# Two-level products in the last two blocks, modulation in place, and a second load of x, in a one-core adaLN + FFN kernel

## The chip, the cores and the metric

The kernel runs on 1 NeuronCore of one Trainium2 chip. The metric is the device time of one execution in microseconds (us). Five engines run their own instruction queues in order: TensorE (PE; its weight loads are listed apart, as PEld), VectorE (DVE), ScalarE (ACT), GpSimd (POOL) and SyncE (SP), which here only issues DMAs. An engine that waits on a semaphore holds up all that is queued behind it.

## The reference

x has 64 batches of 64 rows of 512 (float32), cond has 64 rows of 256.

```python
# modulation and first product
q_emb = relu(q @ W3 + b3)                        # 64 x 512
v_sum = sum(v, axis=1, keepdims=True)            # over the 64 rows of a batch
x1 = (n * v + v_sum) * q_emb[:, None, :]
y  = relu(x1 @ W2 + b2)                          # 4096 x 512 @ 512 x 512
# second product, with a shared and six routed low-rank experts (rank 16, top 2)
base   = y @ W_base + b_base                     # 4096 x 512 @ 512 x 512
shared = (y @ A_s) @ B_s
gates  = softmax(y @ W_router + b_router)        # top 2 of 6, as weights w_per_e
routed = einsum(einsum(y, A_r) * w_per_e, B_r)
out = x + base + shared + routed
```

## The kernel before

Features lie on the 128 partitions (chunks of 128: NC = 4), tokens in the free dimension. The 4096 tokens are cut into NB = 4 blocks (k = 0 to 3) of 1024, a block into two halves h of TB = 512 tokens. Each block has a first product (x1 @ W2, relu to y), then `ph` (y with the 118 columns of A_s, A_r and the router, L801), then `second` (y @ W_base, plus the routed part through `pt`, `hwT` and `bcat_sb`).

Both 512 x 512 products are done by Strassen-Winograd: of the two token halves and two feature halves come 7 products instead of 8. `weight_sums` and `row_sums` make the sums of operands on DVE (`t2`, `tb` for the weights; `s` of the modulated x, `sy` of y); `product(ps, i, j, ...)` is number i of the seven for output chunk j: two matmuls of 128 columns of weights with 512 tokens, accumulated in a PSUM bank. Seven products share four banks named x, y, w and z; what several outputs have in common (p1, u) is carried over by ACT copies and DVE adds. There are six banks for all this (`ps_p`).

- Block 0 (`first_mixed`): the first half of its tokens without Strassen as the data arrives, the rest with seven products.
- Blocks 1 and 2 (`first_seven`): seven products on one level.
- Block 3 (`first_inner`): two levels. Each of the seven products is again done by seven, on 256 tokens (`q(n, t)`): 49 matmuls instead of 28. Here p1, y and z are seeded by ACT copies from PSUM to PSUM (`seed_y`, `seed_z`), and PE adds onto the copy. The sums of the inner level are `inner_t` (weights), and `first`, `sums` and `late` (x); `inner_t`, `first` and `sums` are made during block 2, `late` at the start of block 3.

The order of the work on each engine is the order in which the code issues it (a manual schedule). The modulation of block k+1 is laid between the work of block k by hand: `modulate` makes a list of steps (per chunk a sum over each batch's rows on DVE, then 16 ACT instructions, one for each batch), `prepare` puts these and the row sums of the next block into the list `behind`, `fill(n)` issues the next n steps of it, and `share()`, called nine times in `second`, issues its part of what is left. So an ACT copy or relu that PE waits for may stand behind modulations, and a DVE add behind sums.

`second` first issues the gate (softmax and top 2: three DVE steps, an Exp on ACT, nine DVE steps), then products 1, 6, 7, 2 for j=0, 1, 4, 6, 7 and so on. It takes the residual from x still in SBUF: `add_u` makes u = p1 + y on DVE, and POOL adds x to three copies of it (L662); `add_r` adds product 7; `finish` adds PSUM, bias and the copy with x on DVE (L674) and issues the output DMA on SP.

Pools: three buffers for x, two for v (the modulated x; `inner_s` takes one of them in block 3), one each for `u`, `u22`, `u21`, `u12`, which both products use in turn.

Of the kernel before, what the change touches and what calls it, by code (L numbers as in the profile page):

```python
# [27 lines left out]
NQ = Q // P  # L28
G = E + 1
# [5 lines left out]
def adaln_ffn(ctx: ExitStack, tc: tile.TileContext, xa, x0, x1, head, w3, w2, wb, a, bcat, br, outT):  # L35
# [12 lines left out]
    vpool = ctx.enter_context(tc.tile_pool(name="v", bufs=2))  # L48
    mid = ctx.enter_context(tc.tile_pool(name="mid", bufs=1))
    tmp = ctx.enter_context(tc.tile_pool(name="tmp", bufs=1))  # L50
    tmp1 = ctx.enter_context(tc.tile_pool(name="tmp1", bufs=1))
# [4 lines left out]
    outTv = outT.rearrange("k c h p t -> p c k h t")  # L56
    xs, vs, ss = {}, {}, {}

    def load_x(k):
        xs[k] = xpool.tile([P, NC, 2, TB], F32, tag="x", name=f"x_{k}")  # L60
        for c in range(NC):
            nc.sync.dma_start(xs[k][:, c].rearrange("p h t -> p (h t)"), x1[k - 1, c])
# [4 lines left out]

    def rows(k, f, h):

        return first_rows(f)[:, :, h] if k == 0 else split(xs[k][:, f, h])  # L70

    def split(t, g=2):
        return t.rearrange("p (g n) -> p g n", g=g)
# [50 lines left out]
    load_x(2)  # L124
# [9 lines left out]
    def weight_sums(w, name):  # L134

        b11, b12 = w[:, :KH, :DH], w[:, :KH, DH:]
        b21, b22 = w[:, KH:, :DH], w[:, KH:, DH:]
        all_t = const.tile([P, 4, KH, DH], F32, tag=name, name=name)
        t = [all_t[:, i] for i in range(4)]
        steps = [  # L140
            lambda: nc.vector.tensor_tensor(t[0], b12, b11, ALU.subtract),
            lambda: nc.vector.tensor_tensor(t[1], b22, t[0], ALU.subtract),
            lambda: nc.vector.tensor_tensor(t[2], b22, b12, ALU.subtract),
            lambda: nc.vector.tensor_tensor(t[3], b21, t[1], ALU.subtract),
        ]
        return {1: b11, 2: b21, 3: b22, 4: t[3], 5: t[0], 6: t[1], 7: t[2], "sums": all_t}, steps

# [25 lines left out]
    def modulate(k):  # L173


        vs[k] = v = vpool.tile([P, NC, 2, TB], F32, tag="v", name=f"v_{k}")
        vsum = small.tile([P, NC, BB], F32, tag="vsum", name=f"vsum_{k}")
        nq = small.tile([P, NC, BB], F32, tag="nq", name=f"nq_{k}")

        def sums(c):  # L180
            xc = xs[k][:, c].rearrange("p h (b n) -> p b h n", n=NH)
# [5 lines left out]
        def batches(c, lo, hi):  # L187
            for b in range(lo, hi):
                nc.scalar.activation(  # L189
                    v[:, c, :, ts(b, NH)], xs[k][:, c, :, ts(b, NH)], AF.Identity,  # L190
                    bias=vsum[:, c, b : b + 1], scale=nq[:, c, b : b + 1],
                )

        n = BB // 4
        parts = [(c, lo) for c in range(NC) for lo in range(0, BB, n)]
        steps = [lambda: sums(0)]
        for m, (c, lo) in enumerate(parts):
            if lo == 0 and c + 1 < NC:
                steps.append(lambda c=c, lo=lo: (sums(c + 1), batches(c, lo, lo + n)))
            else:  # L200
                steps.append(lambda c=c, lo=lo: batches(c, lo, lo + n))
        return steps
# [39 lines left out]
    def row_sums(a, name, cols=slice(0, TB)):  # L242

        a11, a12, a21, a22 = a[:, :KH, 0, cols], a[:, KH:, 0, cols], a[:, :KH, 1, cols], a[:, KH:, 1, cols]
        all_s = mid.tile([P, 4, KH, TB], F32, tag=name, name=name)
        s = [all_s[:, i, :, cols] for i in range(4)]
        steps = [
            lambda: nc.vector.tensor_tensor(s[0], a21, a22, ALU.add),
            lambda: nc.vector.tensor_tensor(s[1], s[0], a11, ALU.subtract),
            lambda: nc.vector.tensor_tensor(s[2], a11, a21, ALU.subtract),  # L250
            lambda: nc.vector.tensor_tensor(s[3], a12, s[1], ALU.subtract),
        ]
        return {1: a11, 2: a12, 3: s[3], 4: a22, 5: s[0], 6: s[1], 7: s[2], "sums": all_s}, steps

    def temps(name):
        return {n: tmp.tile([P, KH, TB], F32, tag=n, name=f"{n}_{name}") for n in ("u", "u22", "u21", "u12")}
# [3 lines left out]
    def fill(n):  # L260
        for _ in range(min(n, len(behind))):
            behind.pop(0)()

    def prepare(k):
        behind.extend(modulate(k))
        ss[k], steps = row_sums(vs[k], "s")
        behind.extend(steps)
        if k == NB - 1:
            prepare_inner(k)

    def prepare_inner(k):


        vectors = nc.vector.tensor_tensor
        t_flat = xpool.tile([P, NC, 2, TB], F32, tag="x", name="inner_t").rearrange("p c h t -> p (c h t)")
        at = {i: n for n, i in enumerate((5, 6, 7, 4, 1, 2, 3))}
        inner_t = t_flat[:, : 4 * 7 * P].rearrange("p (n o m) -> p n o m", n=4, o=7)

        def t_of(o, n):
            w, a = t2[o], at[o]  # L280
            b = {1: w[:, 0, :P], 2: w[:, 1, :P], 3: w[:, 1, P:]}
            return b[n] if n in b else inner_t[:, {5: 0, 6: 1, 7: 2, 4: 3}[n], a]

        w_low = w2_sb.rearrange("p (o k) m -> p o k m", k=KH)
        groups = ((slice(0, 4), lambda c, m: t2["sums"][:, :, c, ts(m, P)]),
                  (slice(4, 6), lambda c, m: w_low[:, :, c, ts(m, P)]),
                  (slice(6, 7), lambda c, m: t2[3][:, c, ts(m, P)].unsqueeze(1)))
        t_steps = []
        for o, b in groups:
            t = [inner_t[:, n, o] for n in range(4)]  # L290
            t_steps += [
                lambda t=t, b=b: vectors(t[0], b(0, 1), b(0, 0), ALU.subtract),
                lambda t=t, b=b: vectors(t[1], b(1, 1), t[0], ALU.subtract),
                lambda t=t, b=b: vectors(t[2], b(1, 1), b(0, 1), ALU.subtract),
                lambda t=t, b=b: vectors(t[3], b(1, 0), t[1], ALU.subtract),
            ]
        for n, step in enumerate(t_steps):
            m, other = 2 + n, behind[2 + n]
            behind[m] = lambda step=step, other=other: (other(), step())

        R2 = TB // 2
        s = {}

        def places():
            s["sums"] = vpool.tile([P, NC, 2, TB], F32, tag="v", name="inner_s").rearrange(
                "p c h t -> p (c h t)").rearrange("p (n o t) -> p n o t", n=4, o=4)
            s["first"] = small.tile([P, 4, 1, R2], F32, tag="inner_s1", name="inner_s1")

        def late_places():
            late = mid.tile([P, 4, KH, TB], F32, tag="sy", name="inner_late").rearrange("p n k t -> p (n k t)")  # L310
            s["late"] = late[:, : 8 * R2].rearrange("p (n o t) -> p n o t", n=4, o=2)
            s["e3"] = late[:, 8 * R2 : 12 * R2].rearrange("p (j t) -> p j t", j=KH)

        sources = (("first", lambda c, r: vs[k][:, c, 0, ts(r, R2)].unsqueeze(1)),
                   ("sums", lambda c, r: ss[k]["sums"][:, :, c, ts(r, R2)]),
                   ("late", lambda c, r: vs[k][:, KH + c, :, ts(r, R2)]))
        s_steps = [places]
        for g, a in sources:
            s_steps += [
                lambda g=g, a=a: vectors(s[g][:, 0], a(0, 1), a(1, 1), ALU.add),  # L320
                lambda g=g, a=a: vectors(s[g][:, 1], s[g][:, 0], a(0, 0), ALU.subtract),
                lambda g=g, a=a: vectors(s[g][:, 2], a(0, 0), a(0, 1), ALU.subtract),
                lambda g=g, a=a: vectors(s[g][:, 3], a(1, 0), s[g][:, 1], ALU.subtract),
            ]
        behind.extend(s_steps[:-4])
# [3 lines left out]
        def s_of(o, n):  # L329
# [7 lines left out]
        inner.update(t=t_of, s=s_of, e3=lambda: s["e3"], late=[late_places] + s_steps[-4:])  # L337
# [4 lines left out]
    def first_mixed(y):  # L342
# [3 lines left out]
        vs[0] = v = vpool.tile([P, NC, 2, TB], F32, tag="v", name="v_0")  # L346
# [12 lines left out]
        def without_sums(c):  # L359
            for j in range(KH):  # L360
                nc.tensor.matmul(
                    px[j], w2_sb[:, c, ts(j, P)], v[:, c, 0, other], start=(c == 0), stop=(c % KH == KH - 1),
                    skip_group_check=True,
                )
            if c == KH - 1:
                for j in range(KH):
                    nc.scalar.copy(p1[j], px[j])
# [5 lines left out]
        px = [ps_p.tile([P, cols], F32, tag="pp", name=f"yx_0_{j}") for j in range(KH)]  # L373
        p1 = [mid.tile([P, cols], F32, tag=f"p1_{j}", name=f"p1_0_{j}") for j in range(KH)]
        for c in range(NC):
# [9 lines left out]
            if c == NC - 1:  # L385
                modulate_scalar(v, vsum, nq, c, half, BB)
            if c > 1:
                without_sums(c - 2)
        for f in range(NC):
            nc.scalar.activation(y[:, f, :, :cols], p0[f], AF.Relu, bias=b2_sb[:, f : f + 1])  # L390
        for c in range(NC - 2, NC):
            without_sums(c)
        for step in t2_steps + s_steps:
            step()
        behind.extend(tb_steps)
        prepare(1)
        fill(1)
        for j in range(KH):
            relu(y, j, 0, px[j], other)
        pairs = temps("0")  # L400
        for j in range(KH):
            f1, f2 = j, KH + j
            bank = lambda n: ps_p.tile([P, cols], F32, tag="pp", name=f"y{n}_0_{j}")
            temp = lambda n: pairs[n][:, j, :cols]
            py, pw, pz = bank("y"), bank("w"), bank("z")
            u, r, r1, r2 = temp("u"), temp("u22"), temp("u21"), temp("u12")
            product(py, 6, j, t2, s)
            nc.vector.tensor_tensor(u, py, p1[j], ALU.add)
            product(pw, 5, j, t2, s)
            nc.vector.tensor_tensor(r, pw, u, ALU.add)  # L410
            product(pz, 7, j, t2, s)
# [12 lines left out]
    def first_seven(k, y):  # L424
# [4 lines left out]
        for j in range(KH):  # L429
# [4 lines left out]
            p1 = tmp1.tile([P, TB], F32, tag="p1", name=f"p1_{k}_{j}")  # L434
            u, r, r1, r2 = temp("u"), temp("u22"), temp("u21"), temp("u12")
# [427 lines left out]
```

## Time and profile before

| | |
|---|---|
| three runs, median (lowest, highest) | 265.69 us (265.42, 267.63) |
| the profiled execution | 265.05 us, of which 263.3 us from the first to the last instruction (the span) |
| granted TensorE clock | 0.999 |
| busy: PE, DVE, ACT, POOL | 257.9, 168.4, 119.2, 43.8 us |
| DMA | 20.13 MB moved, 76 GB/s over the span |

The stages on PE, from the chain that ended last (us from the span's start):

| block | first product and ph | second product |
|---|---|---|
| 0 | 5.6 to 40.7 | 40.7 to 72.7 |
| 1 | 72.7 to 104.3 | 104.3 to 136.1 |
| 2 | 136.1 to 167.7 | 167.7 to 199.5 |
| 3 | 199.5 to 228.1 | 228.1 to 259.3, and 4 us of adds and output |

A float32 matmul leaves two records in the trace. Records overlap in the pipeline, so the time that one costs is read from the spacing of starts (the chain's pieces), not from its own duration: four records of 512 columns take 1.72 us, six of 256 columns 1.29 us. The same holds for ACT: a modulation has a mean of 429 ns, but eight in a row take 2.65 us.

### The profile page before, as it was taken

What the parts mean: (1) busy time and instruction counts of PE and PEld (TensorE: products, weight loads), DVE (VectorE), ACT (ScalarE), POOL (GpSimd) and SP (SyncE); (2) the same over time, 40 slices, a digit from 0 to 9 for tenths busy, and PEclk for the clock granted to TensorE, in tenths of its full rate; (3) what the DMA queues carried; (4) which work ended last, traced back from release to release, by engine and by line L of the source; (5) the groups of instructions that cost most, each with busy time, mean ns of one, the idle gap of its engine ahead of it and who ended that gap; (6) DMA issues with size and microseconds to landing.
All of it is one profiled execution on the core that took longest, in us unless ns stands there. A gap on an engine that the chain in (4) does not pass through costs nothing.

```text
span 263.3 us, 2789 instructions
## 1 busy us (share of the span) xinstructions
PE 257.9 (98%) x920; PEld 148.8 (57%) x920; DVE 168.4 (64%) x296; ACT 119.2 (45%) x318; POOL 43.8 (17%) x45
## 2 busy tenths in 40 slices
PE   7999999999999999999999999999999999999995
PEld 3756895454444458444444447744446889845542
DVE  2896889636755448714667776876989566872422
ACT  2499389594018992245003998246004328101000
POOL 1000000570000000435000000055600070045300
PEclk9999999999999999999999999999999999999999
DMA  6999300004362000002220000000332000000323
GB/s 200 364 346 410 123 0 0 0 2 159 115 249 113 0 2 0 1 0 88 111 105 18 0 0 0 2 0 0 113 128 80 1 4 0 0 4 0 120 90 109
DMA packets 10303, 20.13 MB, mean 76 GB/s; under 512 B 1216, under 2 KB 3008, under 8 KB 10288
## 3 DMA queue, kind: packets, MB, share of 16 engines
q1 hardware_dynamic: 10000, 19.82, 20.7%
q8 instruction: 7, 0.11, 0.2%
q10 hardware_dynamic: 288, 0.13, 0.2%
q14 instruction: 8, 0.07, 0.1%
HBM read 11.56 MB, written 8.39 MB: 76 GB/s over the span
## 4 chain that ended last, share of the span: by engine, by line
PE 91%; ACT 5%; DMA 2%; DVE 1%; SPq 0%; issue 0%; DVEq 0%
PE oz L150 11%; PE ox L150 10%; PE ph L801 10%; PE ow L150 9%; PE py L354 5%; PE yw L150 5%; PE yz L150 5%; PE oy L150 5%; PE ia L480 5%; PE ow L668 5%; PE yx L150 4%; PE ib L480 4%; PE yy L150 3%; ACT v L189 3%; PE ox L668 3%; PE oz L668 3%
## 5 line engine op out<-in xcount | busy, mean ns | idle before, releaser
L189 ACT ACTIVATE v<-x,vsum,nq 128x64 f32<-128x64 f32 x192 | 66.3, 429 | 6.7 <-DVE vsum L185 6.7
L662 POOL TENSOR_TENSOR u_o<-u_o,x 128x512 f32<-128x512 f32 x24 | 31.9, 1356 | 178.3 <-DVE u_o L658 178.3
L801 PEld LDWEIGHTS ph<-a_sb,y 128*128 128x128 f32 x256 | 29.5, 192 | 1.8 <-issue 1.0
L801 PE MATMUL ph<-a_sb,y 128*128 128x118 f32 x256 | 29.9, 276 | 0.3 <-ACT y L340 0.3
L150 PE MATMUL ox<-y,wb_sb 128*128 128x512 f32 x64 | 29.5, 593 | 0.0
L340 ACT ACTIVATE y<-u,head_sb 128x512 f32<-128x512 f32 (+1 forms) x26 | 15.9, 633 | 8.8 <-DVE u L412 3.6
L150 PEld LDWEIGHTS ox<-y,wb_sb 128*128 128x128 f32 x64 | 11.8, 190 | 12.9 <-issue 12.9
L674 DVE SCALAR_TENSOR_TENSOR u_o<-ow,head_sb,u_o 128x512 f32<-128x512 f32 x14 | 10.5, 748 | 8.5 <-PE ow L668 8.2
L658 DVE TENSOR_TENSOR u_o<-oy,op 128x512 f32<-128x512 f32 x8 | 5.5, 688 | 15.5 <-PE oy L150 15.5
L354 PE MATMUL py<-v,w_sb 128*128 128x512 f32 (+1 forms) x40 | 14.4, 510 | 0.9 <-DMA w_sb<-in_w_dram 0.9
L150 PE MATMUL oz<-y,tb 128*128 128x512 f32 x32 | 15.1, 595 | 0.0
L150 PE MATMUL yx<-v,w_sb 128*128 128x512 f32 x32 | 15.0, 592 | 0.0
L150 PE MATMUL oz<-sy,tb 128*128 128x512 f32 x32 | 15.0, 592 | 0.0
L150 PE MATMUL oy<-sy,tb 128*128 128x512 f32 x32 | 15.0, 592 | 0.0
L437 ACT COPY p<-yx 128x512 f32<-128x512 f32 x4 | 2.3, 576 | 27.7 <-PE yx L150 27.7
L184 DVE TENSOR_REDUCE vsum<-x 128x16 f32<-128x1024 f32 x12 | 14.5, 1212 | 0.0
L654 ACT COPY op<-ox 128x512 f32<-128x512 f32 x8 | 4.7, 581 | 19.1 <-PE ox L150 19.1
L150 PE MATMUL ow<-sy,tb 128*128 128x512 f32 x28 | 13.2, 593 | 0.0
L150 PE MATMUL ow<-sy,wb_sb 128*128 128x512 f32 x28 | 13.2, 592 | 0.0
L674 DVE SCALAR_TENSOR_TENSOR x<-ox,head_sb,x 128x512 f32<-128x512 f32 x8 | 6.0, 749 | 10.6 <-PE ox L668 10.6
L486 ACT COPY ib<-ia 128x256 f32<-128x256 f32 x7 | 2.5, 357 | 21.2 <-PE ia L480 21.2
L237 ACT ACTIVATE v<-x,vsum,nq 128x64 f32<-128x64 f32 x32 | 10.9, 427 | 1.7 <-DVE vsum L235 1.7
(170 smaller groups left out, 413.3 us busy)
## 6 DMA issues: line engine op xcount, KB each, us to landing
x<-in_x_dram SPq DMA_DIRECT2D x12, 512.0 KB, 7.1
out_dram<-u_o SPq DMA_DIRECT2D x22, 256.0 KB, 2.0
out_dram<-x SPq DMA_DIRECT2D x8, 256.0 KB, 2.1
x<-in_x_dram SPq DMA_DIRECT2D x7, 256.0 KB, 6.0
w_sb<-in_w_dram SPq DMA_DIRECT2D x4, 256.0 KB, 5.7
wb_sb<-in_wb_dram SPq DMA_DIRECT2D x4, 256.0 KB, 5.0
w_sb<-in_w_dram SPq DMA_DIRECT2D x1, 384.0 KB, 4.3
out_dram<-u_o SPq DMA_DIRECT2D x2, 192.0 KB, 1.9
```

Of the source, the lines that this page charges most:

```text
L150: nc.tensor.matmul(ps, w[i][:, c, ts(j, P)], s[i][:, c, :], start=start and c == 0, stop=c == KH - 1, skip_group_check=True,)
L184: nc.vector.tensor_reduce(vsum[:, c, :], xc, AX.XY, ALU.add)
L189: nc.scalar.activation(v[:, c, :, ts(b, NH)], xs[k][:, c, :, ts(b, NH)], AF.Identity, bias=vsum[:, c, b : b + 1], scale=nq[:, c, b : b + 1],)
L237: nc.scalar.activation(v[:, c, :, ts(b, NH)], batches_of(c, b, b + 1)[:, :, 0], AF.Identity, bias=vsum[:, c, b : b + 1], scale=nq[:, c, b ...
L340: nc.scalar.activation(y[:, f, h, cols], src, AF.Relu, bias=b2_sb[:, f : f + 1])
L354: nc.tensor.matmul(p[:, :, lo * NH : hi * NH], w2_sb[:, c, ts(f, P)], v[:, c, :, lo * NH : hi * NH], start=(c == 0 and lo == 0), stop=(c = ...
L480: nc.tensor.matmul(bank[b, t][:, cols], inner["t"](o, n), inner["s"](o, n), start=n == 1, stop=True, skip_group_check=True,)
L658: nc.vector.tensor_tensor(us[j], ps["y", j], p1s[j], ALU.add)
L662: nc.gpsimd.tensor_tensor(split(t[j], x.shape[1]), split(us[j], x.shape[1]), x, ALU.add)
L668: nc.tensor.matmul(ps[name, j], bcat_sb[:, ts(f, P)], hw, start=False, stop=True, skip_group_check=True)
L674: nc.vector.scalar_tensor_tensor(add, split(p, g), bb_sb[:, f : f + 1], add, ALU.add, ALU.add)
L801: nc.tensor.matmul(ph[:, h * NS + s, :HC], y[:, c, h, ts(s, P)], a_sb[:, c, :], start=(c == 0), stop=(c == NC - 1),)
```

## The change

- `first_inner` now serves blocks 2 and 3. `inner_t` gets a place of its own, and its 12 DVE steps are made in block 1's first product (before: block 2's). The inner sums of x run for both blocks.
- While block 2 runs its two-level product, the modulation of block 3 is filled in: 12 units of two ACT instructions each, one or two after each q group. The chunk sums of block 3's modulation are no longer made there, but in the first four units of block 2's list, thus in block 1's first product.
- Modulation writes onto x itself. The v pool goes; x_0's v takes the third x buffer, and x_2, x_3 are loaded when x_0 and v_0 are done with. Units are of two ACT instructions instead of four (33 entries instead of 17 for a block), chunks in the order 0, 2, 1, 3, and the row sums are split by chunk.
- The residual rows are loaded a second time: `load_rows(k)` issues four DMAs of 512 KB after each first product, into the tags `u21`, `u`, `u22`, `u12`. DVE adds PSUM, bias and these rows (`with_x`); POOL's adds of x go.
- `second` seeds bank y from x and bank z from y by ACT copies, as the two-level product does; both products 1 come first, then 6 and 2 for j=0, 7, 6 for j=1, 2, 7, then `pt`; 4 for j=0 comes after it.
- In `first_seven` p1 goes by an ACT copy into bank y, product 6 adds onto it, and so on for z; the order is 1, 5, 6, 2, 7, 3, 4. The last relu reads bank z.
- In block 0 the two halves of px, y, w and z share a bank each, p1 is copied once, a chunk earlier.

```diff
-        vs[k] = v = vpool.tile([P, NC, 2, TB], F32, tag="v", name=f"v_{k}")
+        vs[k] = v = xs[k]
...
+        def batch(c, b):
+            x = v[:, c, :, ts(b, NH)]
+            nc.scalar.activation(x, x, AF.Identity, bias=vsum[:, c, b : b + 1], scale=nq[:, c, b : b + 1])
...
     def prepare(k):
+        if k == NB:
+            return
+        sums, batches = modulation[k]
+        early, late = row_steps(slice(0, 1)), row_steps(slice(1, 2))
+        units = [] if k == NB - 1 else [[sums[CHUNKS[0]]]]
+        for i, c in enumerate(CHUNKS):
+            for b in range(0, BB, 2):
+                unit = batches[c][b : b + 2]
+                if b == 0 and i + 1 < NC and k < NB - 1:
+                    unit.insert(0, sums[CHUNKS[i + 1]])
+                if i == NC - 1 and b % 4 == 2:
+                    unit.append(early[b // 4])
+                units.append(unit)
+        if k == NB - 2:
+            modulation[k + 1] = modulate(k + 1)
+            for n, step in enumerate(list(modulation[k + 1][0].values()) + inner_steps):
+                units[1 + n].append(step)
+        behind.extend(units + [[step] for step in late])
+        if k > 1:
+            behind.extend([step] for step in prepare_inner(k))
...
     def first_seven(k, y):
             product(px, 1, j, t2, s)
-            nc.scalar.copy(p1, px)
-            product(py, 6, j, t2, s)
-            nc.vector.tensor_tensor(u, py, p1, ALU.add)
-            fill(1)
+            nc.scalar.copy(py, px)
             product(pw, 5, j, t2, s)
-            nc.vector.tensor_tensor(r, pw, u, ALU.add)
-            fill(1)
-            product(pz, 7, j, t2, s)
+            nc.scalar.copy(r, pw)
+            product(py, 6, j, t2, s, start=False)
+            nc.scalar.copy(pz, py)
+            product(px, 2, j, t2, s, start=False)
+            nc.scalar.copy(u, py)
+            fill(2)
+            relu(y, f1, 0, px)
+            product(pz, 7, j, t2, s, start=False)
             nc.vector.tensor_tensor(r, pz, r, ALU.add)
+            fill(2)
             relu(y, f2, 1, r)
-            fill(2)
-            product(px, 2, j, t2, s, start=False)
-            relu(y, f1, 0, px)
             product(pw, 3, j, t2, s, start=False)
             nc.vector.tensor_tensor(r2, pw, u, ALU.add)
+            fill(2)
             relu(y, f2, 0, r2)
-            fill(1)
             product(pz, 4, j, t2, s, start=False)
-            nc.vector.tensor_tensor(r1, pz, u, ALU.add)
-            relu(y, f1, 1, r1)
-            fill(1)
+            relu(y, f1, 1, pz)
+            fill(2)
 
     def first_inner(k, y):
+        for step in inner[k]["late"]:
+            step()
+        prepare(k + 1)
...
             take_w5(t)
+            fill(1)
             q(3, t - 1)
             q(6, t)
             seed_z(t)
...
             if order[t - 2] == 2:
                 relus(p1, 0, 0)
+            fill(2 if t in (4, 5) else 1)
...
+    def load_rows(k):
+        res = {}
+        for n, (f, h) in zip(pair_tags[2:3] + pair_tags[:2] + pair_tags[3:], ((1, 0), (1, 1), (0, 0), (0, 1))):
+            res[f, h] = tmp.tile([P, KH, TB], F32, tag=n, name=f"x{n}_{k}")
+            nc.sync.dma_start(
+                res[f, h], x1[k, f * KH : (f + 1) * KH, :, ts(h, TB)].rearrange("c p t -> p c t")
+            )
+        return res
...
+        def seed(name, source, j):
+            nc.scalar.copy(bank(name, j), ps[source, j])
+        def with_x(name, j, f, h):
+            t = row(f, h)
+            nc.vector.scalar_tensor_tensor(t, ps[name, j], bb_sb[:, f : f + 1], t, ALU.add, ALU.add)
+            return t
...
         gate(k, ph)
         prod(1, 0, "x")
-        copy_p1(0)
-        prod(6, 0, "y")
-        add_u(0)
+        seed("y", "x", 0)
+        prod(1, 1, "x")
+        seed("y", "x", 1)
+        prod(6, 0, "y", start=False)
+        seed("z", "y", 0)
+        prod(2, 0, "x", start=False)
...
+        u12[0] = with_x("y", 0, KH, 0)
         share()
-        prod(7, 0, "z")
-        prod(2, 0, "x", start=False)
-        add_r(0)
-        prod(1, 1, "x")
-        copy_p1(1)
+        prod(7, 0, "z", start=False)
+        u22[0] = with_x("z", 0, KH, 1)
+        prod(6, 1, "y", start=False)
+        seed("z", "y", 1)
+        u12[1] = with_x("y", 1, KH + 1, 0)
         share()
...
     for k in range(NB):
-        elif k < NB - 1:
+        elif k == 1:
             first_seven(k, y)
         else:
             rest = first_inner(k, y)
+        res = load_rows(k)
+        if k == 0:
+            load_x(3)
...
-        if k == 0:
-            fill(4)
-        second(k, y, ph)
-        if k + 3 < NB:
-            load_x(k + 3)
+        fill(6 if k else 8)
+        second(k, y, ph, res)
```

## The prediction

> **What bounds the kernel now.** I read the page's busy shares first, then the busy time by stage, the chain that ended last, and last the order of time inside the first products of blocks 2 and 3.
>
> The page: busy time of each engine, and the chain that ended last by engine.
>
> ```profile
> PE 257.9 (98%) x920; PEld 148.8 (57%) x920; DVE 168.4 (64%) x296; ACT 119.2 (45%) x318; POOL 43.8 (17%) x45
> ...
> PE 91%; ACT 5%; DMA 2%; DVE 1%; SPq 0%; issue 0%; DVEq 0%
> ```
>
> TensorE (PE) works 98% of the span, so only less PE work, or less waiting of PE, saves time. Busy time by stage: from the top, the first product and ph (the product with A) of block 1, of block 2, and of block 3; columns: stretch, its length, then busy PE, PE weight load, VectorE (DVE), ScalarE (ACT), GpSimd (POOL), granted clock, DMA share, GB/s.
>
> ```profile
> 72.72:104.31 31.59, 31.43 (x121) 17.85 (x121) 17.74 (x27) 20.80 (x54) 0.00 (x0) 1.00 0.20 75
> 136.12:167.72 31.60, 31.43 (x122) 17.86 (x121) 21.87 (x37) 20.81 (x54) 0.00 (x0) 1.00 0.03 9
> 199.53:228.10 28.57, 28.57 (x164) 25.59 (x163) 20.42 (x41) 13.16 (x34) 5.00 (x4) 1.00 0.04 14
> ```
>
> Block 3, on two levels already, needs 3.03 us less than block 2. The chain in order of time at the end of block 2's first product (start, us, what):
>
> ```profile
> 155.78 0.72 ACT y L340
> 156.50 2.65 ACT v L189 x8
> 159.15 1.19 ACT y L340 x2
> 160.34 1.32 ACT v L189 x4
> 161.66 0.62 ACT y L340
> 162.28 0.04 issue
> 162.32 5.39 PE ph L801 x46
> ```
>
> The last relu (L340) stands behind four modulations (L189), and PE waits for it. A modulation costs 0.33 us start to start (2.65/8, 1.32/4). Order of time in block 3:
>
> ```profile
> 200.47 0.74 DVE L674 SCALAR_TENSOR_TENSOR u_o<-ow,head_sb,u_o 128x512 f32<-128x512 f32 x1
> 203.74 0.42 DVE L471 TENSOR_TENSOR u<-ib,u 128x256 f32<-128x256 f32 x1
> 204.62 0.41 PEld L480 LDWEIGHTS ib<-v,inner_t 128*128 128x128 f32 x2
> ...
> 218.68 1.33 ACT L340 ACTIVATE y<-u,head_sb 128x512 f32<-128x512 f32 x2
> 219.92 1.69 ACT L340 ACTIVATE y<-inner_late,head_sb 128x256 f32<-128x256 f32 x4
> 220.16 1.97 PEld L801 LDWEIGHTS ph<-a_sb,y 128*128 128x128 f32 x16
> ```
>
> Two thin places: a bank is read at 203.74 to 204.16 just before PE writes it again (204.62), and ph meets the relus of inner_late almost as they end.
>
> **1. Block 2 on two levels.** One level: 7 products x 2 column halves x 2 chunks = 28 matmuls of 0.859 us (chain: 1.72 us for four records, two to a matmul) = 24.05. Two levels: 49 matmuls of 0.43 (1.29 us for six records) = 21.04. Less 3.01; by the stages 3.03. Both stages hold 0.4 us of waiting (31.60 - 24.05 - 7.14 for ph = 0.41; 28.57 - 21.04 - 7.14 = 0.39), so I take **-3.03**.
>
> These rows hold half the columns at exactly half the time (0.43 against 0.859), with 0.41 us of weight load per matmul just inside it. The Trainium skill speaks against the step: "TensorE: Matmul & The Clock Gate", section "Back-to-back issue gap", gives a stream of weight loads and matmuls about 81 ns at 128 columns and 131 at 512, far from proportional; an estimate between them puts 256 columns at three quarters of 512, and 49 matmuls at 31 us, 7 us lost. The rows decide.
>
> **2. ScalarE in block 2.** New there: 12 units of two modulations of block 3, 24 x 0.33 = 8 us on an engine busy 13.2 of 28.6 us. Laid into block 3's order of time, the pairs and fours between the PSUM seeds put off the later seeds by 0.3 to 0.5 us, and the tightest of them still ends 0.25 us before PE wants it. The unit that follows the relus of p1 delays those of inner_late by 0.67; ph takes the second of them, ready at 219.92 + 0.85 = 220.77, at about 220.9, so 0.13 is slack: **+0.55**. Bounds: 0 and 0.8 (with 0.43, the mean of a lone modulation).
>
> **3. Block 1's first product.** The last relu now reads PSUM directly, without the DVE add, and stands ahead of the fill: it ends about 1.0 us after the product, and ph needs it only after 16 records (1.8 us). So the 0.41 of waiting goes: **-0.41**. Each p1 now passes through an ACT copy into the bank that product 6 adds to. For j=0 the copy (0.58) lies beside product 5 (1.72). For j=1 ACT's queue is late: counted from the block's start, product 7 of j=0 ends at 8.6, its add takes 0.61, and then two chunk sums of block 3, moved here, at 1.41 each (the chunk sums at 32.12 and 33.87 take 1.41 to 1.42 with their two small steps) occupy DVE till 12.05; the next add ends at 12.75, relus 12.8 to 14.0, four modulations to 15.35, the copy to 15.95. PE wants it after product 5 of j=1, at 9 x 1.717 = 15.45: **+0.5** (bounds 0.2, 1.0). The rest of the 19 us that DVE gets here (sums, weight sums) fits into its idle time.
>
> **4. Block 3's start.** In block 2's second product the modulations spread over more shares, and output x1 moves ahead of w1: the row sums, which DVE had all done by 190.5, now end with three (0.6 each) after the w1 output, and that is ready 23.2 us after ph instead of 21.5. Adding DVE's queue from there (rows of 190 to 203: 0.6 for 512 columns, 1.14 to 1.25 for 1024, 0.66 for an output, 0.4 for 256): the last output ends 34.4 after ph, the four late sums 37.0, which is 5.2 after block 3's start; in the rows shown it was 203.74 - 199.53 = 4.2. The 0.42 us read follows, and PE's write waits: 1.0 late less 0.46 of slack, **+0.5** (bounds 0, 1.0). Block 2's start has the same queue with less ACT behind it: 4.0, nothing.
>
> **5. Block 0.** PE waited 0.28 (22.56 to 22.84) for a copy of p1 behind the last modulations. The copy now comes a chunk earlier, and two matmul pairs move ahead of chunk 3; the row sums come 0.6 later, and the first product that needs them starts as they end: **-0.25** (bounds -0.3, +0.2).
>
> **6. Second products, everything else.** PE's matmuls are the same in number. Four ACT seeds of 0.58 replace two copies; each lies beside a whole product (1.72), except the first, which stands behind the gate's Exp. DVE has the same number of passes (8 outputs with x and bias, 4 adds). The 24 POOL adds (31.9 us) fall away; they were off the path, but row sums took 1.7 to 2.3 us beside them instead of 1.22. The loads of x, 4 x 512 KB a block, stand in SP's queue after the former block's outputs; a 512 KB load landed 7.1 us after issue, the last is issued as the first product ends, the first use is DVE's after hw, 13 us after it. x_2 waits for x_0's last modulation (23 us) and x_3 for v_0 (34 us); they are read after 72. The row tiles' outputs are out before their tags are written again: the tightest, u21, lands 3.7 us into block 2 and is written at 6.4. In-place modulation waits for nothing new. At the end an add without bias replaces one with: under 0.1. **0**.
>
> **Sum:** -3.03 + 0.55 - 0.41 + 0.5 + 0.5 - 0.25 = -2.14. The profiled execution took 265.05, so 262.9. The runs shown lay above it, the lowest by 0.37, the median by 0.64; with 0.4 of that I say **263.3**, 0.9% under the median.
>
> **Rivals.**
> *The waits of 2 to 4 are hidden.* Each is a few tenths worked out of queue positions; DVE without POOL beside it may run its queue earlier. Then -3.03 - 0.41 - 0.25 = -3.7: 261.35, 261.75 with the 0.4. For: each rests on 0.1 to 0.5 us of slack. Against: ACT's order in 2 is fixed.
> *The gate holds the seeds (slower).* In all four blocks the first seed, and with it the third product, stands behind Exp on ACT, which waits for DVE: four row sums of y (4.7), in blocks 0 and 1 a chunk sum (1.41), three gate steps (0.7). Before, the second product waited for no copy. By the rows, the seed is ready 0.2 us early in block 0, 1.8 in block 1, 0.65 in block 2, 0.8 in block 3 (block 3: the row of Exp at 229.85, copy done at 230.57, wanted at 231.39). If the chain is 1.5 us later than counted, PE loses 1.3 + 0 + 0.85 + 0.7 = 2.85: 265.75, 266.15 as run, slower than before. It decides from about 1.2 us of delay. For: no cover left in block 0. Against: DVE loses POOL's interference.
> *More waits of the kind in 3 and 4.* At their upper bounds (0.8, 1.0, 1.0, +0.2): -0.4, thus 264.6 to 265.1.
> *The change does not halve anything.* If block 2 did not copy block 3's rate; the rows of block 3 exclude nearly all of it.
>
> **Chances.** Forecast 0.48, hidden waits 0.26, more waits 0.14, gate 0.10, others 0.02. 1%, about what a measurement of this kernel can tell from no change, is 263.0 below and 268.3 above; the forecast's own spread (0.5) puts a third of it under 263.0. Faster 0.43, same 0.50, slower 0.07 (a gate chain later than 2.5 us). The range takes the hidden waits with 0.5 to spare and the upper bounds: 261.2 to 265.3, leaving out the gate.
>
> **What would show it.** Block 2 to the end of ph at 29.1 instead of 31.6, with some 0.5 us between 8 and 16 records into ph; a wait of PE for an ACT copy into yy between j=0 and j=1 of block 1, and none before ph; a wait of PE for DVE 5 us into block 3; no wait in the second products. Wrong if an ox or oy load waits for ACT in each block (gate), if 128x256 records in block 2 stand further apart than 0.215, or if DVE waits for loads of x.

## The result, and the profile after

The changed kernel took **263.36 us** (median of seven runs, 263.01 to 263.46) against 265.69 before: a ratio of 0.988, 95% interval 0.985 to 0.992. A second set, beside the experiments, gave 263.18 (263.09 to 263.50) and 0.991 (0.989 to 0.994). The forecast was 263.3, in a range of 261.2 to 265.3. The profiled execution took 263.01 us, of which 261.2 is the span; before it was 265.05 and 263.3.

The page of the changed kernel: busy time by engine, and the chain that ended last by engine.

```profile
PE 255.4 (98%) x962; PEld 156.5 (60%) x962; DVE 175.3 (67%) x335; ACT 133.5 (51%) x355; POOL 16.9 (6%) x25
...
PE 93%; ACT 2%; DVE 2%; DMA 2%; SPq 0%; issue 0%; DVEq 0%
```

PE still sets the time. Its own work fell by 2.5 us, the share of ScalarE (ACT) in the chain fell from 5% to 2%, and POOL lost its adds (43.8 to 16.9 us). VectorE (DVE) and ACT are busy for longer than before (175.3 after 168.4 and 133.5 after 119.2 us). That as such costs nothing; three places in their queues do, as shown below.

Busy time by stage of the changed kernel: from the top the first product and ph of block 1, of block 2 and of block 3, in the columns of the prediction's table (stretch, length, busy PE, PE weight load, DVE, ACT, POOL, granted clock, DMA share, GB/s).

```profile
72.59:104.66 32.07, 31.45 (x122) 17.70 (x121) 23.95 (x45) 23.36 (x58) 0.00 (x0) 1.00 0.21 74
136.46:165.62 29.16, 29.00 (x163) 25.73 (x163) 20.12 (x41) 24.53 (x70) 5.01 (x4) 1.00 0.24 80
197.43:226.18 28.75, 28.75 (x163) 25.51 (x163) 21.03 (x42) 13.16 (x34) 5.00 (x4) 1.00 0.24 83
```

Block 2 lost 2.44 us, block 1 got 0.48 longer, block 3 0.18. All stages, from the chain in order of time:

| stage | before | after | difference | predicted |
|---|---|---|---|---|
| start of the first product | 5.75 | 5.90 | +0.15 | 0 |
| block 0, first product and ph | 34.93 | 34.89 | -0.04 | -0.25 |
| block 0, second product | 32.04 | 31.80 | -0.24 | 0 |
| block 1, first product and ph | 31.59 | 32.07 | +0.48 | -0.41 + 0.5 |
| block 2, first product and ph | 31.60 | 29.16 | -2.44 | -3.03 + 0.55 |
| block 3, first product and ph | 28.57 | 28.75 | +0.18 | +0.5 |
| blocks 1 and 2, second products | 63.62 | 63.61 | -0.01 | 0 |
| block 3, second product and the rest | 35.20 | 35.02 | -0.18 | under 0.1 |

The sum of the differences is -2.10, the prediction's -2.14. That the sum comes out so well is luck, because errors cancel: 0.8 us too much in some rows, 0.75 too little in others.

Where block 1 lost time: the chain that ended last, in order of time (start, us, what).

```profile
81.27 0.69 DVE u L451
...
82.05 1.13 DVE vsum L204
...
83.46 1.13 DVE vsum L204
...
84.79 0.70 DVE u L455
...
85.52 1.30 ACT y L344 x2
86.82 1.32 ACT x L209 x4
88.14 0.49 ACT yy L441
...
88.67 1.98 PE yy L170 x4
...
97.52 7.14 PE ph L814 x64
```

This is step 3 of the prediction, link by link: an add, two chunk sums of block 3 (`vsum`), the next add, two relus, four modulations, the copy into bank y, and PE behind it. The last line shows the other half of the step: ph takes 7.14 us, its bare 64 records, so the wait for the last relu is gone.

Block 2, order of time at the end of its first product (in brackets: idle time before, and what ended it).

```profile
156.85 0.76 ACT L209 ACTIVATE x<-x,vsum,nq 128x64 f32<-128x64 f32 x2
...
157.51 1.69 ACT L344 ACTIVATE y<-inner_late,head_sb 128x256 f32<-128x256 f32 x4
158.06 1.59 PEld L814 LDWEIGHTS ph<-a_sb,y 128*128 128x128 f32 x12 [0.34 <-ACT y L344]
```

The unit of two modulations stands ahead of the four relus of `inner_late`. After its first four records ph waits for the first of these relus (the row at 158.06), and two records later, until 158.46, for the second.

Block 3, order of time five us after its start.

```profile
202.33 0.41 DVE L476 TENSOR_TENSOR u<-ib,u 128x256 f32<-128x256 f32 x1
...
202.80 0.30 PEld L485 LDWEIGHTS ib<-x,inner_t 128*128 128x128 f32 x2 [0.31 <-DVE u L476]
```

Bank ib is read 4.90 us after the start of the block (before: 4.21), and PE's write waits for that read, as step 4 said, but for a shorter time.

### The profile page after: what moved, and what is told of

Same layout as the page of the kernel before. It is cut to its first block, busy times and chain, and to the rows that moved or that the text cites. A ratio compares the mean times of both kernels' runs of the same rounds, so it can differ in the third digit from the quotient of the medians.

```text
span 261.2 us, 2959 instructions
## 1 busy us (share of the span) xinstructions
PE 255.4 (98%) x962; PEld 156.5 (60%) x962; DVE 175.3 (67%) x335; ACT 133.5 (51%) x355; POOL 16.9 (6%) x25
## 4 chain that ended last, share of the span: by engine, by line
PE 93%; ACT 2%; DVE 2%; DMA 2%; SPq 0%; issue 0%; DVEq 0%
PE ph L814 11%; PE ox L170 11%; PE oz L170 11%; PE ow L170 9%; PE ia L485 9%; PE ib L485 7%; PE py L358 5%; PE oy L170 5%; PE ow L677 5%; PE yz L170 3%; PE yw L170 3%; PE ox L677 3%; PE oz L677 3%; PE yy L170 2%; PE yx L170 2%; DMA w_sb<-in_w_dram 2%
## 5 line engine op out<-in xcount | busy, mean ns | idle before, releaser
L209 ACT ACTIVATE x<-x,vsum,nq 128x64 f32<-128x64 f32 x192 | 66.8, 431 | 0.0
L673 DVE SCALAR_TENSOR_TENSOR xu<-oz,head_sb,xu 128x512 f32<-128x512 f32 x16 | 12.0, 749 | 16.9 <-PE oz L170 14.2
L344 ACT ACTIVATE y<-u,head_sb 128x256 f32<-128x256 f32 (+1 forms) x26 | 14.4, 600 | 8.4 <-DVE u L417 3.9
L476 DVE TENSOR_TENSOR u<-ib,u 128x256 f32<-128x256 f32 x28 | 11.1, 421 | 9.9 <-PE ib L485 9.9
L741 POOL TENSOR_TENSOR hwd<-hwT 112x512 f32<-112x512 f32 x4 | 5.9, 1464 | 172.5 <-ACT hwT L739 172.5
L476 DVE TENSOR_TENSOR u<-ia,u 128x256 f32<-128x256 f32 (+1 forms) x24 | 10.8, 464 | 3.7 <-ACT u L523 2.2
L698 DVE TENSOR_TENSOR xu<-ow,xu 128x512 f32<-128x512 f32 x14 | 9.6, 687 | 5.4 <-PE ow L677 5.1
L665 ACT COPY oz<-oy 128x512 f32<-128x512 f32 x8 | 4.6, 570 | 16.9 <-PE oy L170 16.9
L673 DVE SCALAR_TENSOR_TENSOR xu<-ox,head_sb,xu 128x512 f32<-128x512 f32 x8 | 6.0, 748 | 10.5 <-PE ox L677 10.5
L247 ACT ACTIVATE v<-x,vsum,nq 128x64 f32<-128x64 f32 x32 | 11.0, 428 | 1.6 <-DVE vsum L245 1.6
```

Source lines behind the costliest of these rows:

```text
L209: nc.scalar.activation(x, x, AF.Identity, bias=vsum[:, c, b : b + 1], scale=nq[:, c, b : b + 1])
L247: nc.scalar.activation(v[:, c, :, ts(b, NH)], batches_of(c, b, b + 1)[:, :, 0], AF.Identity, bias=vsum[:, c, b : b + 1], scale=nq[:, c, b ...
L344: nc.scalar.activation(y[:, f, h, cols], src, AF.Relu, bias=b2_sb[:, f : f + 1])
L476: add = lambda o, a, b: nc.vector.tensor_tensor(o, a, b, ALU.add)
L673: nc.vector.scalar_tensor_tensor(t, ps[name, j], bb_sb[:, f : f + 1], t, ALU.add, ALU.add)
L698: nc.vector.tensor_tensor(add[:, cols], p[:, cols], add[:, cols], ALU.add)
```

## The experiments

Each kernel ran beside the kernel before on the same chip; only the late sums split ran beside the changed kernel too, in their second set. The relu behind the modulations, the two kernels with a later gate, the residual loads twice and POOL's additions ran once each; the others are medians of 4 to 10 runs. The length of a block is always that of its first product and ph.

### Block 2 on one level

```diff
-        elif k == 1:
+        elif k < NB - 1:
             first_seven(k, y)
...
-        if k > 1:
+        if k == NB - 1:
             behind.extend([step] for step in prepare_inner(k))
```

> Block 2's first product goes back to seven products on one level (28 matmuls of 512 tokens); all else stays as changed. Theory (the gain is PE's matmul work in block 2, less a wait in its ph): block 2 to the end of ph is 24.05 + 7.14 = 31.2 us instead of 29.16, so the time rises by 2.0 (1.8 to 2.3), to 265.0 to 265.4. No new wait between j=0 and j=1, since block 3's chunk sums are still made in block 1. Rival (the gain comes from POOL, from the loads or from the second products): the time stays within 0.5 us of 263.4.

Measured: 265.21 us, ratio 0.999 (0.998 to 1.000): nearly all of the gain is gone. Block 2 took 31.18, 2.02 more than in the changed kernel, and block 3 28.57, as before. The two add up to 1.84 us, which is what the kernel lost against 263.36. The chain of this run at the start of block 2, at its ph, and behind it:

```profile
136.76 1.72 PE yx L170 x4
...
160.80 7.14 PE ph L814 x64
167.94 3.44 PE ox L170 x8
```

So two levels in block 2 carry the change; the rest of it, gains and the wait in block 1 together, comes to next to nothing. They also bring the wait in block 3: with one level in block 2 it does not arise.

### The sums of block 3 later, no unit ahead of the late relus, and both

The chunk sums of block 3 move from the units 1 to 4 of block 2's list to the units 22 to 25:

```diff
-                units[1 + n].append(step)
+                units[22 + n if n < NC else 1 + n].append(step)
```

No unit in the last round of the two-level product, so none ahead of the relus of `inner_late`:

```diff
-            fill(2 if t in (4, 5) else 1)
+            if t < 6:
+                fill(2 if t in (4, 5) else 1)
```

> The four chunk sums of block 3 move from units 1 to 4 of block 2's list (block 1's first product) to units 22 to 25 (block 1's second product). Theory (two of them stand on DVE between the adds of products 7 and 3 and so put off relus, modulations and the copy that PE waits for): PE's wait for the copy into yy goes, block 1 to the end of ph is 31.2 us instead of 32.07, the time falls by 0.85 (0.7 to 0.95), and block 1's second product stays at 31.8. Rival (ACT's own queue, with two copies more per j and the modulations, is what is late): the wait keeps at least 0.5 us.

> The one unit (two modulations) after the relus of p1, at t = 6, is not issued in the two-level product; it moves to the second product. Theory: the relus of inner_late come 0.67 us earlier in block 2 and ph of block 2 no longer waits: block 2 to the end of ph is 28.6 us instead of 29.16, the time falls by 0.55 (0.4 to 0.6). Rival (the 24 modulations in the two-level product delay seeds all along, and ph shows only the end of it): the stage falls by less than 0.25.

> The two edits before together. Theory: their gains add, 1.4 us (1.1 to 1.55) less than the changed kernel, about 262.0, since they act on different stages. Rival (ACT or DVE is short of time as a whole, and what is moved out of one stage is late in the next): less than 0.8 us.

Measured, against 32.07, 29.16 and 28.75 in the changed kernel:

| | us | ratio to before | block 1 | block 2 | block 3 |
|---|---|---|---|---|---|
| sums later | 262.54 | 0.989 (0.987 to 0.991) | 31.17 | 29.16 | 28.75 |
| no unit there | 262.72 | 0.990 (0.988 to 0.991) | 32.07 | 28.58 | 28.75 |
| both | 262.18 | 0.988 (0.986 to 0.990) | 31.17 | 28.57 | 28.75 |

Each edit takes away one wait and changes no other stage of blocks 1 to 3 by more than 0.04 us: 0.90 us with the chunk sums moved (two of the four stood ahead of the add), 0.58 without the unit ahead of the relus. The chain shows it: PE behind the copy in block 1 with the sums later, and ph in block 2 with no unit there.

```profile
88.14 1.72 PE yy L170 x4
...
157.92 1.78 PE ph L815 x16
```

This shows the causes of steps 2 and 3, not only their sizes. Block 1 has now no wait left: its length is its busy time, 31.17. From the changed kernel's profiled execution (263.01) to that of "both" (261.91) the fall is 1.10 us where the stages say 1.48: block 0's ph ended at 41.16 us after 40.79, 0.37 later.

### The late sums of block 3 split

```diff
-        for step in inner[k]["late"]:
+        late = inner[k]["late"]
+        for step in late[:3]:
             step()
...
             take_1(t - 2)
+            if t == 2:
+                for step in late[3:]:
+                    step()
```

> On e4_both (sums later, no two units in the seventh group), with one more edit: of block 3's and block 2's four late inner sums of x, three stay ahead of the inner product and the fourth is made after its third group's first product. Theory (the wait of 0.18 us in block 3 is the last row sums and late sums on VectorE holding the read of bank ib): block 3's first product and ph go from 28.75 to 28.57, all other stages stay as in e4_both (block 1 31.17, block 2 28.57, second products 31.8), so 0.18 less than e4_both. Rival (the wait is the bank's own turn, whatever VectorE has queued): 28.75 stays, no change.

Measured: 262.16 us (261.46 to 263.57), ratio 0.987 (0.984 to 0.991). The first entry of `late` only opens their places, so the edit leaves two of the four late sums ahead (not three, as was expected) and moves two, in blocks 2 and 3; in block 3 they start at 202.01 us, behind the read of bank ib (201.26). Block 3 took 28.57 instead of 28.75, the other stages were as foretold. The single runs differ by 2 us. In the profiled one (262.45) the chain waits for loads of x until 20.5 us and block 0's ph ends at 41.89; in that of the second set (261.36) it is 19.4 and 40.77. This fits a start that varies with the loads; the other runs have no trace. The second set ran beside the changed kernel on one chip:

> The kernel after, unchanged, on the same chip as g2: 263.4 us, stages as in its first trace (block 1 32.07, block 2 29.16, block 3 28.75).

> The same kernel as e5_late_split, beside the kernel after on one chip: by the stages 0.90 less in block 1, 0.58 in block 2, 0.18 in block 3, 1.66 us in all, so 261.7 us if the start of the work (which moves by up to 1 us with the arrival of the first loads) is the same on the mean. Rival (the gains of the stages are taken back at the start or the end): less than 1 us under the kernel after.

Measured: the changed kernel 263.18 us (263.09 to 263.50), this one **261.49** (261.36 to 261.99), 1.69 us less where the stages say 1.66. Against the kernel before: 0.985 (0.982 to 0.988). It is faster than both the kernel before and the changed kernel. Busy time by stage of this kernel, blocks 1, 2 and 3:

```profile
72.57:103.74 31.17, 31.17 (x121) 17.77 (x121) 18.41 (x33) 23.43 (x58) 0.00 (x0) 1.00 0.22 76
135.54:164.11 28.57, 28.57 (x164) 25.59 (x163) 20.19 (x41) 23.94 (x68) 5.00 (x4) 1.00 0.26 85
195.92:224.49 28.57, 28.57 (x164) 25.59 (x163) 21.17 (x42) 13.16 (x34) 5.00 (x4) 1.00 0.23 82
```

PE counts as busy for the whole of each stretch. In block 2 ACT has modulations of block 3 to do (23.94 us busy against 13.16 in block 3), and the block takes exactly as long as block 3 without them: this load of the engine costs nothing, while the place of two instructions in its queue cost 0.58 us.

### The relu behind the modulations again

On the kernel with the sums later and no unit there ("both"):

```diff
             product(pz, 4, j, t2, s, start=False)
-            relu(y, f1, 1, pz)
             fill(2)
+            relu(y, f1, 1, pz)
```

> On e4_both (no seed wait in block 1), with one edit: in block 1's first product the last relu of a chunk stands behind the two units of modulation issued with it again, as it did in the kernel before. Theory (the 0.41 us that ph waited for in block 1 of the kernel before went because the relu moved ahead of the modulations): block 1's first product and ph go from 31.17 to between 31.45 and 31.65, with TensorE waiting for ScalarE's relu inside ph; all other stages as in e4_both. Rival (the wait went because the last relu reads PSUM and needs no VectorE add): 31.17 stays within 0.1.

Measured: 262.30 us; block 1 31.45, +0.28. Order of time at the end of block 1's first product:

```profile
97.09 1.42 ACT L209 ACTIVATE x<-x,vsum,nq 128x64 f32<-128x64 f32 x4
98.41 0.67 ACT L344 ACTIVATE y<-yz,head_sb 128x512 f32<-128x512 f32 x1
...
99.14 4.99 PEld L815 LDWEIGHTS ph<-a_sb,y 128*128 128x128 f32 x44 [0.20 <-ACT y L344]
```

The wait in ph is back, so most of the 0.41 us that the change saved there came from the order, relu first. The remaining 0.13 was not tested by itself; the DVE add that the kernel before had ahead of its relu lies in the same place.

### The gate later

```diff
         fill(6 if k else 8)
+        for _ in range(2):
+            steps()[0]()
         second(k, y, ph, res)
```

> The kernel after, with two redundant passes of 128x1024 (the first of the row sums of y again, 1.14 us start to start) on VectorE ahead of the gate of every block: work added, nothing left out. The gate's chain comes 2.28 us later. Theory (the first seed of the second product stands behind Exp, and has the margins that the trace of after shows: about 0.3, 0.9, 0.7 and 0.8 us in blocks 0 to 3): TensorE waits 2.0, 1.4, 1.6 and 1.5 us at the start of the second products, 6.5 us in all, 269.5 us. By the margins of the prediction (0.2, 1.8, 0.65, 0.8) it would be 2.1, 0.5, 1.6 and 1.5, 5.7 us in all. Rival (seed and Exp do not set it, the order of products has cover): within 0.5 us of the kernel after.

Measured: 271.59 us, span 269.8, 8.3 more than the changed kernel's 261.5 in its second set. PE stood 2.01, 0.35, 1.55 and 1.48 us in blocks 0 to 3. In blocks 1 to 3 the four records after the wait took 1.98 instead of 1.72, 0.26 more. With 0.26 for each wait this is 2.3, 0.6, 1.8 and 1.7; by the prediction's margins the waits were to be 2.1, 0.5, 1.6 and 1.5. The margins that the prediction read from the kernel before were better than mine from the trace after: in block 1 the copy waits for the product that it copies (idle 0.82 us behind Exp), not for Exp, and I had counted from the copy. The four make 6.4; the rest is in block 0. Order of time there, and then four short stretches of it (granted clock: third number from the end):

```profile
46.67 2.83 PE L170 MATMUL oy<-sy,tb 128*128 128x512 f32 x4 [2.01 <-ACT oy L665]
49.30 2.77 PE L170 MATMUL ox<-y,wb_sb 128*128 128x512 f32 x4
```

```profile
44.50:46.60 2.10, 0.17 (x1) 0.00 (x0) 1.69 (x6) 0.71 (x3) 0.00 (x0) 1.00 1.03 420
...
47.80:48.40 0.60, 0.60 (x1) 0.13 (x1) 0.56 (x2) 0.00 (x0) 0.00 (x0) 0.50 1.03 410
...
50.20:50.80 0.60, 0.60 (x2) 0.29 (x1) 0.60 (x2) 0.60 (x3) 0.00 (x0) 0.50 0.00 0
...
51.40:52.00 0.60, 0.60 (x3) 0.28 (x2) 0.00 (x0) 0.60 (x3) 0.00 (x0) 1.00 0.00 0
```

After the wait of 2.01 us the granted clock fell to a half, from about 47.7 to 51.1, 3.4 us, which costs another 1.7. After the other three waits it stayed at 1.00. Longer waits, by three such passes instead of two (`range(3)`), show whether their length decides that:

> As f2_gate_later, with three redundant passes ahead of the gate instead of two: 1.14 us more wait of TensorE in each block, so waits of some 3.2, 1.7, 2.7 and 2.6 us at the start of the second products instead of 2.0, 0.6, 1.55 and 1.5: span 269.8 + 4.6 = 274.4 us by the waits alone. Theory (a wait of TensorE of 2 us or more costs a further 1.7 us each time, as in block 0 of f2_gate_later, where the granted clock fell to a half for 3.4 us afterwards): half clock after the waits of blocks 0, 2 and 3, none or one after that of block 1, span 277.8 us. Rival (the half clock there was a matter of how the wait lay, once): half clock in block 0 at most, span near 274.4 us.

Measured: span 280.5, more than either expected. The waits were 3.27, 1.62, 2.81 and 2.74 us. Stretches from the end of each wait, blocks 0 to 3:

```profile
47.80:56.20 8.40, 8.37 (x13) 3.65 (x14) 4.36 (x9) 3.04 (x8) 0.00 (x0) 0.64 0.16 62
116.50:121.90 5.40, 5.38 (x13) 2.51 (x14) 4.26 (x9) 3.03 (x8) 0.00 (x0) 1.00 0.00 0
180.50:187.40 6.90, 6.83 (x13) 3.13 (x14) 4.36 (x10) 3.07 (x9) 0.00 (x0) 0.78 0.00 0
245.50:254.00 8.50, 8.45 (x13) 3.61 (x14) 4.36 (x9) 1.05 (x3) 0.00 (x0) 0.63 0.00 0
```

In the two runs together the half clock followed all four waits of 2.01 us or more and none of the four of 1.62 us or less. Here it costs 3.0, 1.5 and 3.1 us (length by one less the clock), so 6.0, 3.0 and 6.3 us of work at half speed. The theory holds for which waits, its size was too small.

In this run the half clock began before the waits ended. In shorter stretches the granted clock is 0.95 over 46.50 to 47.00 us, 0.73 over 179.70 to 180.50 and 0.68 over 244.60 to 245.50, and at the end 0.78 over 53.60 to 54.00, 0.76 over 183.20 to 183.80 and 0.79 over 251.50 to 252.10. With 0.50 and 1.00 as the only values, the clock was a half from 46.95 to 53.78, from 180.07 to 183.49 and from 244.92 to 251.75: 6.83, 3.42 and 6.83 us, or two, one and two steps of 3.413. The three starts lie 133.12 and 64.85 us apart, 39 and 19 such steps. So the clock seems to change only at a fixed beat, and the idle time between two beats to count: cut by that beat, the four waits that were followed by half clock have 2.01 to 2.39 us in one step, the others at most 1.55. This is worked out from two runs; no run moves a wait against the beat.

The Trainium skill, "TensorE: Matmul & The Clock Gate", section "What's actually happening", states two states, a half clock and the full one, and windows of about 3.4 us that run free of the kernel. The two values 0.50 and 1.00, the 3.4 us and the beat agree with the numbers above. It asks for an idle window of 3.4 us before the clock falls, and its section "HAM oscillation — how this bites in real kernels" for no gap above that; here a wait of 2.01 us was enough, so the rows decide.

### The residual loads twice

```diff
-            nc.sync.dma_start(...)
+            for _ in range(2):
+                nc.sync.dma_start(...)
```

> The kernel after, with each residual load issued twice in a row (8 MB more from HBM): work added, nothing left out. Theory (the second load of x is hidden: 512 KB lands some 4 to 8 us after issue and the first use is after hw, 9 us or more behind the last issue): time as the kernel after within 0.3 us. Rival (DMA time counts: the outputs and loads of x behind it in SP's queue, or VectorE's output adds, are held): VectorE waits for DMA in the second products and the time grows by 1 us or more.

Measured: 263.37 us; 36.9 MB instead of 28.5 went through the queues, a load of 512 KB landed in 3.8 us (4.1 in the changed kernel), the second products took 31.80 and DVE waited for none of the rows. So the second load of x is hidden, as step 6 said, and even twice that load is.

### POOL's additions back, off the path

```diff
+        def pool_adds(t):
+            for n in range(3):
+                junk = small.tile([P, TB], F32, tag="junk", name=f"junk_{k}_{n}")
+                nc.gpsimd.tensor_tensor(junk, t, y[:, n, 0, :], ALU.add)
...
         u12[0] = with_x("y", 0, KH, 0)
+        pool_adds(u12[0])
```

(and the same after `u12[1]`.)

> The kernel after, with six additions of 128x512 on GpSimd in every block again (24, as the kernel before had), of an output row and y into a tile that nobody reads, issued after the first two outputs of the second product: work added, nothing left out. Theory (GpSimd's additions slow VectorE's passes beside them, which the kernel before showed as 1.7 to 2.3 us for sums that take 1.22 alone): VectorE's passes in the second products take 1.3 to 2 times as long while GpSimd runs, its busy time grows by 5 to 15 us, and the time by 0 to 0.5 us, since it is off the path. Rival (GpSimd does not disturb VectorE, the longer sums had another cause): durations on VectorE as in the kernel after.

Measured: 263.19 us, stages as in the changed kernel; DVE busy 179.7 us, 4.4 more. Order of time in block 1's second product of this kernel, and last a row sum of the changed kernel at the same place:

```profile
116.64 4.62 POOL L710 TENSOR_TENSOR junk<-xu,y 128x512 f32<-128x512 f32 x3 [1.31 <-DVE xu L673]
118.53 0.75 DVE L673 SCALAR_TENSOR_TENSOR xu<-oz,head_sb,xu 128x512 f32<-128x512 f32 x1 [1.43 <-PE oz L170]
119.20 0.94 DVE L261 TENSOR_TENSOR s<-s,x 128x512 f32<-128x512 f32 x1
120.06 1.76 DVE L262 TENSOR_TENSOR s<-x 128x512 f32<-128x512 f32 x1
...
119.71 0.68 DVE L262 TENSOR_TENSOR s<-x 128x512 f32<-128x512 f32 x1
```

The row sums take up to 1.76 us beside POOL instead of 0.68; an output that reads a PSUM bank (0.75) is as fast as without POOL (0.75). So POOL does disturb DVE, as in the kernel before, but by less in sum than expected (5 to 15 us) and at no cost in time: by this run, 24 such adds take some 4.4 us of an engine that has them to spare. The Trainium skill, "SBUF — State Buffer", section "Who interferes with whom", says that a DVE instruction contends with a GpSimd instruction that reads SBUF if both of its inputs are in SBUF, and not if only one is. The four rows of this kernel agree.

## Why the prediction was right, point by point

**1. Two levels in block 2 (-3.03).** Right in sum. One level without a wait takes 31.18 (block 2 on one level), two levels 28.57 (no unit ahead of the late relus): 2.61; the other 0.42 of the 3.03 was the wait that the one-level stage had in the kernel before, which the new one-level product would have lost too. The bare count, 3.01, was thus too much: both stages were said to hold 0.4 us of waiting, and only the one-level stage could lose its own. What the two-level stage has is at its start, before and after: ten records take 2.30 us (six take 1.29) and four 1.00 (elsewhere 0.86), behind ACT copies (L500 and L494 of the changed kernel), and no edit here touches that. The rows of block 3 were the right witness: half the columns at half the time, with modulations on ACT beside them or without (28.57 in both blocks).

**2. ACT in block 2 (+0.55).** Right in cause and size: 0.58 with the unit, 0 without. The place was off: the wait was to come between 8 and 16 records into ph, and it came after the fourth and the sixth.

**3. Block 1 (-0.41 and +0.5).** The first half right: ph takes 7.14. The second is the term that was mis-sized: the cause is the one named, shown by moving the sums, but it costs 0.90. Each link ended a little later than I counted (the copy at 16.04 after the block's start, not 15.95; PE stood 0.62), and I left out what PE loses beyond the wait itself: 0.26, seen in the four records of 1.98 us, here and after the waits of the runs with a later gate at full clock.

**4. Block 3's start (+0.5).** The wait is there, by the read named, and goes when two of the late sums are moved behind it. Its size was 0.18: the read came 4.90 after the start, not 5.2, and all but 0.18 of its 0.69 us of delay was slack.

**5. Block 0 (-0.25).** Half wrong; block 0 gained 0.04. The wait of 0.28 for the copy went, but a new one of 0.12 came, and one of 0.20 where the kernel before had 0.07. Chain in order of time of the changed kernel, block 0:

```profile
24.69 0.98 PE yy L170 x4
...
31.73 1.06 PE yw L170 x4
```

Four records of 256 columns take 0.86; both pieces begin with a wait. I had seen the first ("starts as they end") and counted it as nothing; the second, for an add of DVE, was not in the prediction. Both are read from the chain; no run moves either.

**6. Everything else (0).** Right for the loads, the copies and the blocks 1 and 2. Missed: a wait of the kernel before in block 0's second product, from its order of time:

```profile
48.49 0.69 DVE L665 TENSOR_TENSOR u_o<-oz,u_o 128x512 f32<-128x512 f32 x1 [0.40 <-POOL u_o L662]
...
49.23 0.30 PEld L150 LDWEIGHTS oz<-y,tb 128*128 128x128 f32 x2 [0.79 <-DVE u_o L665]
```

I wrote that the POOL adds "were off the path". In three blocks they were; in block 0 a DVE add waited for one of them, and PE, which was to write the same bank, for the add. It cost 0.24 and went with POOL's adds. This is argued from the two rows; no run restores that dependence.

**The rivals.** That the waits are hidden fell: all three came. Nor were they all at their upper bounds: 0.58, 0.90 and 0.18 where 0.8, 1.0 and 1.0 were the bounds. The gate did not hold the seeds: PE stands nowhere at a seed of the second products. The runs with a later gate show that this rival was real, at a price above mine: margins as counted, but 0.26 more for each wait and, after the waits of 2.01 us and more, the half clock.

**The offset.** The profiled execution of the changed kernel was again under the median, by 0.35; I had taken 0.4.

## What to carry to other kernels

Where one engine is busy for 98% of the span, price the work that goes from it by rows of the same shape elsewhere in the kernel, and then follow every queue that the change refills up to the next instruction that this engine waits for: here the product gave 2.6 us, and three misplaced groups of small instructions took 1.66 back, which three small edits then recovered. Count for each new wait not only the lateness but what comes on top of it, 0.26 us in the streams of 512 columns here, and keep waits of TensorE short: those of up to 1.62 us left the clock alone here, those from 2.01 us on did not. Of each operation that is removed "off the path", ask once per block who waits for it.

## What the runs showed of the hardware that I had not expected

- Waits of TensorE of 2.01, 2.74, 2.81 and 3.27 us were each followed by 3.0 to 6.3 us of work at a granted clock of 0.50; waits of 0.35, 1.48, 1.55 and 1.62 us by none. Where it turns stays open. The half clock began and ended at a beat of 3.41 us, so when the wait begins should matter as well; no run tests that by itself.
- A wait of TensorE between products of 512 columns cost 0.26 us beyond itself (four records 1.98 instead of 1.72 us).
- Twice the residual traffic (8.4 MB more) moved no stage of blocks 1 to 3 by more than 0.02 us (one run).
